# Token term of a graph layer: two small matmul groups on TensorE, or rows gathered from a table in DRAM

## The chip, the core and the metric

The kernel runs on one core of one Trainium2 chip. The metric is the device time of one execution in microseconds (us). TensorE is called PE in the profile, VectorE is DVE, ScalarE is ACT, GpSimd is POOL, and SyncE (SP) issues the kernel's transfers.

## The reference, cut to what matters

There are 64 sequences of 256 tokens, 768 wide. The adjacency is 0 or 1 with a mean of 1/64.

```
h    = relu(layernorm(x))
deg  = adj.sum(-1);  rdeg = adj.sum(1)            # both directions
ctx  = adj @ (h Wadj' + badj) / max(deg,1) + adj' @ (h Wrev' + brev) / max(rdeg,1) + h Wself' + bself
rel  = deg * (E[1] Wr' + br) + rdeg * (E[41] Wrr' + brr)      # for adjacencies of 0 and 1
out  = x + ctx + rel
```

For one token, everything that isn't a product with `h` is a sum of five rows of 768 elements: `badj` if deg > 0, `brev` if rdeg > 0, `bself`, deg times one vector, and rdeg times another. This is the token term. It depends on the two degrees alone.

## The kernel before

A sequence has two blocks of 128 tokens (c = 0, 1). The three weight products are computed in float32r words by a scheme of 15 products instead of 18 (`PRODUCTS`), in two sweeps over the sequences: sweep 1 runs 8 products for each of the 62 regular sequences and stores the partial blocks to DRAM (`kept`); sweep 2 loads them, runs the other 7 products and the aggregation with the adjacency, and stores the output. Sequences 0 and 63 are irregular: their products are taken whole, in full precision, at the start and at the junction of the sweeps. The junction also prepares the second set of weight words.

`record` writes every operation into a `Plan` with an engine, a planned duration and a rank; `Plan.schedule` is a list scheduler that runs at build time and fixes the order on each engine. The ranks are moved by a table of `OFFSETS`, one per kind of operation. Large tiles of 128x768 live in 18 rotating buffers (class B). All transfers go through SP's one queue. Engines work in order.

The parts around the change:

- `front1` (sweep 1): layernorm's statistics end in 4 columns of a tile `cols`: mean and variance of each block; GpSimd takes the power -1/2 (L721). TensorE turns the tile (L724), ScalarE copies 4 rows out of PSUM (L727), SP stores them to a DRAM tile `d` (L731) and loads them back broadcast as `row` (L734), with which GpSimd and VectorE normalise the transposed tokens (L743, L747).
- `rows_prepare` (at the junction): builds a tile `rows` of the five token-term rows, high and low parts, four times in groups of 32 partitions.
- `front2` (sweep 2): ScalarE converts the adjacency and sums the degrees (L896); VectorE writes indicator and degree columns into `cols` (L908, L909); TensorE turns them (L913); ScalarE copies them to `token` (L917).
- `add_rows` (L638): four matmuls with 32 rows each, on four row groups of TensorE, add the token term into the PSUM banks of products 7 and 15 (chains v and u), which are then read by VectorE into blocks (0, 1) and (1, 1). In the irregular sequences it has banks of its own, and VectorE adds them (L979).
- `product` reads a bank into the blocks it feeds (L685, L687); `high_low` splits finished blocks for the aggregation (ScalarE L926, GpSimd L930); `aggregate` multiplies (L942) and VectorE adds the result, divided by the degree, into blocks (c, 1) (L953).
- `split` makes the three words of a left operand (ScalarE L600, VectorE L613 and L617), from sums that GpSimd makes (L590).
- `flag`: a general path runs if any adjacency value is neither 0 nor 1.

## Time and profile before

| | |
|---|---|
| three timed runs | 2492.59, 2494.84, 2495.69 us (median 2494.84) |
| profiled execution, span | 2494.7 us |
| TensorE busy | 2467.6 us, 99% |
| VectorE, ScalarE, GpSimd busy | 84%, 72%, 52% |
| transfers | 590.67 MB, mean 237 GB/s, all on SP's queue |

The span reaches from the first to the last instruction of the profiled execution; its own device time isn't listed apart, and the span is within 0.1% of the runs. Busy time counts an engine's instructions, not its waits. Matmuls are pipelined, so a row's duration overlaps the next one; differences of start times tell what a group takes.

### The profile page before, as it was taken

Reading aid. Unit: us, or ns where it says so; the run is one execution under the profiler, and the core shown is the slowest. Engines: PE = TensorE matmul, PEld = TensorE weight load, DVE = VectorE, ACT = ScalarE, POOL = GpSimd, SP = SyncE. Lnnn points to the kernel's source line nnn. Section 1 sums busy time; section 2 is a strip of 40 time slices with the busy share of each in tenths; the row PEclk is TensorE's granted clock in tenths of the full one; section 3 lists DMA queues with packets and bytes.
Section 4 is the critical chain, followed back from the end, with each engine's and each line's share of the span. In section 5 each row is a group of like instructions: output and inputs, shape, how many; then the busy total and the mean of one; then the engine's idle time right before and its main releaser. Section 6 shows DMA issues by size and latency. Waiting matters only on the chain.

```text
span 2494.7 us, 43472 instructions
## 1 busy us (share of the span) xinstructions
PE 2467.6 (99%) x13922; PEld 2381.1 (95%) x13922; DVE 2091.7 (84%) x3939; ACT 1787.1 (72%) x3836; POOL 1285.3 (52%) x1138
## 2 busy tenths in 40 slices
PE   7999999999999999999999999999999999999998
PEld 4899999999999999996999999999999999999998
DVE  7887787777777777778988988888888888888887
ACT  3788888888888888886666666666666666666664
POOL 1555555555555555552555555555555555555554
PEclk9999999999999999999999999999999999999999
DMA  5677777777777677776666666666666666666663
GB/s 211 235 285 266 269 281 268 268 277 271 267 282 278 260 276 282 276 274 231 209 215 216 213 212 213 213 214 213 214 214 215 215 215 216 215 215 215 213 219 130
DMA packets 224009, 590.67 MB, mean 237 GB/s; under 512 B 24056, under 2 KB 24312, under 8 KB 223776
## 3 DMA queue, kind: packets, MB, share of 16 engines
q1 hardware_dynamic: 223776, 587.86, 67.3%
q8 instruction: 110, 1.80, 0.3%
q14 instruction: 123, 1.01, 0.1%
HBM read 364.28 MB, written 223.48 MB: 236 GB/s over the span
## 4 chain that ended last, share of the span: by engine, by line
PE 96%; DMA 1%; DVE 1%; ACT 1%; issue 0%; POOL 0%; SPq 0%; DVEq 0%; ACTq 0%; POOLq 0%
PE x L628 21%; PE y L628 20%; PE agg L942 14%; PE z L628 10%; PE w L628 10%; PE t L628 5%; PE v L628 5%; PE u L628 5%; PE whole L780 2%; PE v L638 1%; DMA raw<-in_Wadj_dram 0%; DMA raw<-in_Wself_dram 0%; PE right L502 0%; PE pt L724 0%; DVE right L555 0%
## 5 line engine op out<-in xcount | busy, mean ns | idle before, releaser
L930 POOL TENSOR_TENSOR hl<-c,hl 128x768 fp32r<-128x768 f32 x256 | 475.3, 1857 | 649.3 <-ACT hl L926 459.2
L628 PE MATMUL x<-word,left 128*128 128x384 f32 x2976 | 592.2, 340 | 0.2 <-DVE c L687 0.2
L628 PE MATMUL y<-word,left 128*128 128x384 f32 x2976 | 573.1, 337 | 0.0
L628 PEld LDWEIGHTS x<-word,left 128*128 128x128 f32 x2976 | 517.4, 188 | 14.2 <-issue 11.0
L628 PEld LDWEIGHTS y<-word,left 128*128 128x128 f32 x2976 | 521.4, 188 | 5.3 <-ACT y L666 0.6
L942 PE MATMUL agg<-hl,a 128*128 128x384 f32 x2048 | 395.4, 335 | 0.0
L743 POOL TENSOR_TENSOR h<-h,row 128x768 f32<-128x768 f32 x128 | 235.7, 1863 | 266.5 <-DMA row<-d 217.3
L942 PEld LDWEIGHTS agg<-hl,a 128*128 128x128 f32 x2048 | 358.5, 188 | 0.5 <-issue 0.2
L628 PE MATMUL w<-word,left 128*128 128x384 f32 x1488 | 304.2, 339 | 1.4 <-DVE x L791 1.3
L628 PE MATMUL z<-word,left 128*128 128x384 f32 x1488 | 301.3, 337 | 0.2
L666 ACT ACTIVATE x<-x 128x768 f32<-128x768 f32 x248 | 191.8, 794 | 140.1 <-PE x L628 139.9
L628 PEld LDWEIGHTS z<-word,left 128*128 128x128 f32 x1488 | 260.4, 188 | 3.4 <-ACT c L676 0.4
L628 PEld LDWEIGHTS w<-word,left 128*128 128x128 f32 x1488 | 258.3, 188 | 4.5 <-DVE x L791 1.6
L953 DVE SCALAR_TENSOR_TENSOR c<-agg,rd,c 128x768 f32<-128x768 f32 x252 | 255.0, 1012 | 7.3 <-PE agg L942 4.0
L926 ACT ACTIVATE hl<-c 128x768 fp32r<-128x768 f32 x256 | 215.1, 841 | 32.1 <-DVE c L685 24.3
L666 ACT ACTIVATE y<-y 128x768 f32<-128x768 f32 x248 | 197.3, 796 | 44.4 <-PE y L628 44.4
L617 DVE SCALAR_TENSOR_TENSOR left<-left,top 128x256 fp32r<-128x256 f32 x496 | 199.2, 412 | 6.3
L617 DVE SCALAR_TENSOR_TENSOR left<-left 128x256 fp32r<-128x256 f32 x434 | 203.0, 489 | 0.1
L685 DVE TENSOR_TENSOR c<-c,v 128x768 f32<-128x768 f32 x124 | 117.3, 946 | 101.5 <-PE v L628 100.5
L607 ACT ACTIVATE top<-left 128x256 f32<-128x256 f32 x496 | 181.2, 383 | 6.6 <-DVE left L617 2.6
L721 POOL TENSOR_TENSOR cols<-cols,half 128x2 f32<-128x2 f32 x64 | 83.9, 1311 | 152.9 <-DVE cols L720 152.9
L676 ACT ACTIVATE c<-y 128x768 f32<-128x768 f32 x124 | 100.9, 814 | 71.7 <-PE y L628 71.7
(138 smaller groups left out, 4343.8 us busy)
## 6 DMA issues: line engine op xcount, KB each, us to landing
c<-kept SPq DMA_DIRECT2D x316, 384.0 KB
kept<-c SPq DMA_DIRECT2D x252, 384.0 KB
x<-in_x_dram SPq DMA_DIRECT2D x128, 384.0 KB
h<-in_x_t_dram SPq DMA_DIRECT2D x128, 384.0 KB
out_dram<-c SPq DMA_DIRECT2D x126, 384.0 KB
kept_h<-h SPq DMA_DIRECT2D x124, 384.0 KB
h<-kept_h SPq DMA_DIRECT2D x124, 384.0 KB
adj<-in_adj_dram SPq DMA_DIRECT2D x64, 512.0 KB
```

Of the source, the lines that this page charges most:

```text
L607: lambda: nc.scalar.activation(view(top), t(w)[:, 0].bitcast(F32), AF.Copy),
L617: lambda: nc.vector.scalar_tensor_tensor(t(w)[:, 2], t(w)[:, 1].bitcast(F32), -STEP, first(), op0=ALU.mult, op1=ALU.add), s == 1,
L628: nc.tensor.matmul(t(q)[:, half, : H // 2], t(w)[:, lw, f, :], t(r[rw])[:, f, ts(half, H // 2)], start=start and i == 0 and f == 0, stop=s ...
L666: lambda: nc.scalar.activation(view(), view(), AF.Copy, scale=scale),
L676: lambda o=o, sign=sign: nc.scalar.activation(t(o).rearrange("p (k n) -> p k n", k=2), view(), AF.Copy, scale=sign * (1.0 if value_last el ...
L685: emit = lambda to=to, op=op: nc.vector.tensor_tensor(to(), to(), view(), op=op)
L721: pool(0.7, r - 21.5, f"pow {b}", [col], [col], lambda: nc.gpsimd.tensor_tensor(var(), var(), v["half"], op=ALU.pow))
L743: lambda h=h, one=one: nc.gpsimd.tensor_tensor(t(h), t(h), one(0), op=ALU.subtract),
L926: lambda: nc.scalar.activation(t(pair)[:, 0], t(o), AF.Copy, scale=LOWER),
L930: lambda: nc.gpsimd.tensor_tensor(t(pair)[:, 1], t(o), t(pair)[:, 0].bitcast(F32), op=ALU.subtract),
L942: nc.tensor.matmul(t(q)[:, half, : H // 2], t(s["a"])[:, c, k, ts(ic, P)], t(pairs[c])[:, part, ts(half, H // 2)], start=(c == 0 and part ...
L953: lambda q=q, to=to, ic=ic: nc.vector.scalar_tensor_tensor(to(), t(q)[:, :, : H // 2], t(rd)[:, ic, k : k + 1], to(), op0=ALU.mult, op1=AL ...
```

## The change

The token term comes from a table in DRAM of 1024 rows, one for each pair of degrees below 32. `table_prepare` builds it during sweep 1, from the fifth sequence on, one step for each of 12 sequences (`PACE_TABLE` is 17 us): the two weight vectors by matmuls, the bias rows loaded broadcast to 128 partitions, 14 VectorE operations on 128x768, and 8 stores of 128 rows. In `front2`, VectorE makes a row number 32 deg + rdeg for each token (place, index), and for each of the two blocks GpSimd issues an indirect transfer that adds the 128 rows numbered by the index to block (c, 1) in SBUF. The token columns, their turn, their copy, the token-row matmuls and `rows_prepare` go. The reads of the banks of products 7 and 15 no longer wait for the rows.

The statistics are turned by VectorE, which transposes 32x32 squares: the four columns stand 8 apart in a tile of 128x32, and the store to `d` picks every eighth partition. The general path also runs if a degree is 32 or more. The planner gets the gather's planned times (1.2 us on GpSimd and on the queue, 3.5 us to land), and the `OFFSETS` are replaced as a whole (not shown).

```diff
+SPAN = 32
...
+PACE_TABLE = 17.0
+GATHER = 3.5
...
+                elif o.name.startswith("gather"):
+                    idle[e] = o.end
+                    queue = max(queue, now) + 1.2
+                    o.end += GATHER
...
-    def add_rows(b, rank, token, qs, start):
...
-        pe(0.55, rank, f"token rows {b}", [token, v["rows"], *qs], [*qs], run)
...
-        if s == 0 or n not in (7, 15):
-            for i in range(len(reads)):
-                read(i)
-            return
-        read(0)
-        return q, lambda: read(1)
+        for i in range(len(reads)):
+            read(i)
...
+        four = lambda: t(col).rearrange("p (c k e) -> p c k e", c=C, k=2)[:, :, :, 0]
...
-        pt = plan.buf("U", None, None, f"pt_{b}", inside=hold)
-        line = plan.buf("S", [P, P], F32, f"line_{b}")
-        pe(0.3, r - 20.0, f"turn {b}", [col], [pt], lambda: nc.tensor.transpose(t(pt)[:, :P], t(col), v["ident"]))
-        act(
-            0.27, r - 19.5, f"line {b}", [pt], [line],
-            lambda: nc.scalar.activation(t(line)[:4], t(pt)[:4, :P], AF.Copy),
-        )
+        line = plan.buf("S", [P, 32], F32, f"line_{b}")
+        dve(0.17, r - 19.5, f"line {b}", [col], [line], lambda: nc.vector.transpose(t(line), t(col)))
         d = plan.buf(None, None, None, "d", v["dram"].tile([4, P], F32, tag="d", name=f"d_{b}"))
         row = plan.buf("A", [P, 4, P], F32, f"row_{b}")
-        dma(2, r - 19.0, f"d {b}", [line], [d], lambda: nc.sync.dma_start(t(d), t(line)[:4]))
+
+        def spread():
+            nc.sync.dma_start(
+                t(d).rearrange("k (q j) -> q k j", q=4), t(line).rearrange("(m e) j -> m e j", e=8)[:, 0]
+            )
+
+        dma(2, r - 19.0, f"d {b}", [line], [d], spread)
...
+    def table_prepare(rank):
+        table = v["table"]
+        pick = plan.buf("B", [P, H], F32, "pick")
         wr = [plan.buf("B", [P, H], F32, f"wr{k}") for k in range(2)]
+        vec = [plan.buf("B", [P, H], F32, f"vec{k}") for k in range(2)]
+        base = plan.buf("B", [P, H], F32, "base")
+        rev = plan.buf("B", [P, H], F32, "rev")
+        fwd = plan.buf("B", [P, H], F32, "fwd")
+        cols = plan.buf("S", [P, 16], F32, "table_cols")
+        for q in range(P // SPAN):
+            at = slice(SPAN * q, SPAN * (q + 1))
+
...
+            pool(0.6, rank - 9.0, "count", [], [(cols, q)], count)
...
         dma(40, rank - 8.0, "eT", [], [(pick, 9)], lambda: nc.sync.dma_start(t(pick)[:, 2 * P : 2 * P + NREL], v["e_t"]))
+        step = PACE_TABLE
         for k in range(2):
+            dma(384, rank - 8.0 + step * k, "wr", [], [wr[k]], lambda k=k: nc.sync.dma_start(t(wr[k]), v["wr"][k]))
+        for i, (r, to) in enumerate(((3, vec[0]), (4, vec[1]), (2, base), (1, rev), (0, fwd))):
+            dma(
+                384, rank - 7.0 + step * i, "bias", [], [to],
+                lambda r=r, to=to: nc.sync.dma_start(t(to), v["bias"][r].partition_broadcast(P)),
+            )
...
+        for k in range(2):
+            pr = plan.buf("Q", [P, 2, 512], F32, f"pr{k}")
+
+            def picks(k=k, pr=pr):
+                for n in range(2):
                     nc.tensor.matmul(
+                        t(pr)[:, n, : H // 2], t(pick)[:, k * P : (k + 1) * P], t(wr[k])[:, ts(n, H // 2)], start=True, stop=True
                     )
 
+            pe(1.45, rank - 4.0 + step * k, "pick", [(pick, k), wr[k]], [pr], picks)
+            dve(
+                on_dve(H), rank - 3.0 + step * k, "vec", [pr, vec[k]], [vec[k]],
+                lambda k=k, pr=pr: nc.vector.tensor_tensor(
+                    t(vec[k]).rearrange("p (k n) -> p k n", k=2), t(vec[k]).rearrange("p (k n) -> p k n", k=2),
+                    t(pr)[:, :, : H // 2], op=ALU.add,
+                ),
+            )
+
+        def add(name, at, one, col, to, out=None):
+            out = out or to
+            dve(
+                on_dve(H), at, name, [one, cols, to], [out],
+                lambda: nc.vector.scalar_tensor_tensor(
+                    t(out), t(one), t(cols)[:, col : col + 1], t(to), op0=ALU.mult, op1=ALU.add
+                ), True,
+            )
+
+        add("base", rank + 2.0 * step, vec[1], 8, base)
+        add("base", rank + 3.0 * step, rev, 9, base)
+        for i in range(SPAN * SPAN // P):
+            tile_ = plan.buf("B", [P, H], F32, f"table{i}")
+            at = rank + (4.0 + i) * step
+            if i == 0:
+                add(f"table {i}", at, fwd, 10, base, tile_)
+                add(f"table {i}", at, vec[0], i, tile_)
+                dve(
+                    on_dve(H), at + 1.0, "base", [base, fwd], [base],
+                    lambda: nc.vector.tensor_tensor(t(base), t(base), t(fwd), op=ALU.add), True,
+                )
+            else:
+                add(f"table {i}", at, vec[0], i, base, tile_)
+            dma(
+                384, at + 2.0, "table", [tile_], [(table, i)],
+                lambda tile_=tile_, i=i: nc.sync.dma_start(t(table)[ts(i, P), :], t(tile_)),
+            )
...
-        col, rd = v["cols"][b % 2], v["rd"][b % 2]
+        rd = v["rd"][b % 2]
         degs = [(deg, (b, c, k)) for c in range(C) for k in range(2)]
...
-        dve(0.2, r - 2.0, f"tok {b}", degs, [(col, 0)], lambda: nc.vector.tensor_scalar(to(0), of(), 0.0, None, op0=ALU.is_gt))
-        dve(0.2, r - 2.0, f"tok {b}", degs, [(col, 1)], lambda: nc.vector.tensor_copy(to(3), of()))
+        place = plan.buf("S", [P, 2 * C], F32, f"place_{b}")
+        index = plan.buf("S", [P, C], I32, f"index_{b}")
+        dve(
+            0.2, r - 2.0, f"place {b}", degs, [place],
+            lambda: nc.vector.tensor_scalar(
+                t(place), t(deg)[:, b].rearrange("p c k -> p (c k)"), 0.0, float(SPAN - 1), op0=ALU.max, op1=ALU.min
+            ),
+        )
+
+        def index_of():
+            one = lambda k: t(place).rearrange("p (c k) -> p c k", k=2)[:, :, k]
+            nc.vector.scalar_tensor_tensor(t(index), one(0), float(SPAN), one(1), op0=ALU.mult, op1=ALU.add)
+
+        dve(0.2, r - 1.5, f"index {b}", [place], [index], index_of)
         dve(0.2, r - 2.0, f"rd {b}", degs, [rd], lambda: nc.vector.tensor_scalar(t(rd), t(deg)[:, b], 1.0, None, op0=ALU.max))
         dve(0.2, r - 2.0, f"rd {b}", [rd], [rd], lambda: nc.vector.reciprocal(t(rd), t(rd)))
-        pt = plan.buf("Q", [P, 2, 512], F32, f"pt2_{b}")
-        pe(0.3, r - 1.0, f"turn2 {b}", [col], [pt], lambda: nc.tensor.transpose(t(pt)[:, 0, :P], t(col), v["ident"]))
-        s["token"] = v["tokens"][b % 2]
...
+        for c in range(C):
+            o = blocks[b, c, 1]
+            plan.op(
+                "POOL", 1.2, r + 1.0 + 2.0 * c, f"gather{c} {b}", [index, o, v["table"]], [o],
+                lambda o=o, c=c: nc.gpsimd.indirect_dma_start(
+                    t(o), None, t(v["table"]), IndirectOffsetOnAxis(ap=t(index)[:, c : c + 1], axis=0), compute_op=ALU.add
+                ),
+            )
         return s
...
-        held = []
         for i, spec in enumerate(SWEEPS[1] if b in regular else ()):
-            more = product(b, 1, spec, r + 2.1 * i, banks)
-            if more:
...
-        if b not in regular:
...
+            product(b, 1, spec, r + 2.1 * i, banks)
...
+        table_prepare(start1[4])
         front1(B - 1)
         whole(B - 1, 1, last)
-        rows_prepare(last + 20.0)
...
+        dve(
+            0.5, start2[B - 2] + 1.0, "rest", [deg, rest], [deg],
+            lambda: nc.vector.tensor_scalar(t(deg), t(deg), float(SPAN), None, op0=ALU.is_ge),
+        )
+        most = plan.buf("S", [P, 1], F32, "most")
         dve(0.4, start2[B - 2] + 1.0, "total", [rest], [total], lambda: nc.vector.tensor_reduce(t(total), t(rest), AX.XY, ALU.add))
+        dve(
+            0.5, start2[B - 2] + 1.0, "total", [deg], [most],
+            lambda: nc.vector.tensor_reduce(t(most), t(deg).rearrange("p b c k -> p b (c k)"), AX.XY, ALU.add),
+        )
+        dve(
+            0.2, start2[B - 2] + 1.0, "total", [total, most], [total],
+            lambda: nc.vector.tensor_tensor(t(total), t(total), t(most), op=ALU.add),
+        )
...
-            "cols": [own(f"cols{i}", [P, P], F32) for i in range(2)],
-            "tokens": [own(f"token{i}", [P, P], F32R) for i in range(2)],
+            "cols": [own(f"cols{i}", [P, 32], F32) for i in range(2)],
+            "table": plan.buf(None, None, None, "table", keep.tile([SPAN * SPAN, H], F32, name="table")),
```

## Rows read from the trace of the kernel before

**Rows 1.** The page's part 1, busy us (share of the span) xinstructions.

```profile
PE 2467.6 (99%) x13922; PEld 2381.1 (95%) x13922; DVE 2091.7 (84%) x3939; ACT 1787.1 (72%) x3836; POOL 1285.3 (52%) x1138
```

**Rows 2.** The page's part 4, the chain that ended last, by engine.

```profile
PE 96%; DMA 1%; DVE 1%; ACT 1%; issue 0%; POOL 0%; SPq 0%; DVEq 0%; ACTq 0%; POOLq 0%
```

**Rows 3.** Windows of one sequence: PE, PEld, DVE, ACT, POOL busy, clock, DMA share, GB/s.

```profile
130.00:146.90 16.90, 16.90 (x99) 16.82 (x98) 13.42 (x30) 14.17 (x29) 8.87 (x9) 1.00 0.74 277
...
1556.00:1576.90 20.90, 20.90 (x123) 20.43 (x122) 18.48 (x33) 13.48 (x33) 10.95 (x9) 1.00 0.65 214
```

**Rows 4.** TensorE in order of time, sweep 2: start us, us, engine, line.

```profile
1555.06 1.55 PE L942 MATMUL agg<-hl,a 128*128 128x384 f32 x8
...
1570.36 0.27 PE L913 MATMUL pt<-ident,cols 128*128 128x128 f32 x1
...
1571.89 0.85 PE L628 MATMUL u<-word,left 128*128 128x384 f32 x4
1572.58 1.55 PE L942 MATMUL agg<-hl,a 128*128 128x384 f32 x8
1574.06 0.44 PE L638 MATMUL v<-rows,token 32*128 32x384 f32 x2
...
1575.95 1.55 PE L942 MATMUL agg<-hl,a 128*128 128x384 f32 x8
```

**Rows 5.** Line 638: duration ns min/median/max, first and last start us.

```profile
L638 PE MATMUL v<-rows,token x124: 434/436/439, 1201.3 to 2473.2; 32*128 32x384 f32 x124
```

**Rows 6.** TensorE in order of time, sweep 1.

```profile
1085.07 0.87 PE L628 MATMUL z<-word,left 128*128 128x384 f32 x4
1085.78 0.27 PE L724 MATMUL pt<-ident,cols 128*128 128x128 f32 x1
...
1086.59 1.58 PE L628 MATMUL y<-word,left 128*128 128x384 f32 x8
```

**Rows 7.** TensorE in order of time, the junction.

```profile
1159.75 0.96 PE L638 MATMUL rows<-rows,token 32*128 32x384 f32 x4
1160.64 5.43 PE L780 MATMUL whole<-raw,h 128*128 128x384 f32 x16
```

**Rows 8.** All engines in order of time, the start.

```profile
6.74 0.71 POOL L721 TENSOR_TENSOR cols<-cols,half 128x2 f32<-128x2 f32 x1 [5.42 <-DVE cols L720]
...
8.30 0.34 SPq L731 DMA_DIRECT2D d<-line  x1
...
11.41 0.36 SPq L734 DMA_DIRECT2D row<-d  x1
```

**Rows 9.** Groups by line: busy us, mean ns of one, idle before.

```profile
L930 POOL TENSOR_TENSOR hl<-c,hl 128x768 fp32r<-128x768 f32 x256 | 475.3, 1857 | 649.3 <-ACT hl L926 459.2 <-DMA c<-in_x_dram 176.9 <-issue 13.2
...
L617 DVE SCALAR_TENSOR_TENSOR left<-left 128x256 fp32r<-128x256 f32 x434 | 203.0, 489 | 0.1
...
L720 DVE TENSOR_SCALAR cols<-cols 128x2 f32<-128x2 f32 x64 | 10.6, 165 | 1.0
```

**Rows 10.** Lines 617 and 721: duration ns min/median/max, first and last start.

```profile
L617 DVE SCALAR_TENSOR_TENSOR left<-left x434: 396/414/787, 1175.9 to 2472.3; 128x256 fp32r<-128x256 f32 x145
...
L721 POOL TENSOR_TENSOR cols<-cols,half x64: 699/1340/1383, 6.7 to 1103.3; 128x2 f32<-128x2 f32 x64
```

**Rows 11.** All engines in order of time, sweep 2, around the degrees.

```profile
1564.41 0.19 ACT L896 ACTIVATION_READ_ACCUMULATOR a<-adj 128x1 f32 x1
...
1568.36 0.17 DVE L908 TENSOR_SCALAR cols<-deg 128x16 f32<-128x16 f32 x1
...
1570.62 0.95 DVE L685 TENSOR_TENSOR c<-c,v 128x768 f32<-128x768 f32 x1 [1.73 <-PE v L628]
...
1572.09 0.96 DVE L687 SCALAR_TENSOR_TENSOR c<-x,c 128x768 f32<-128x768 f32 x1 [0.52 <-PE x L628]
```

**Rows 12.** All engines in order of time, sweep 1, around one broadcast.

```profile
124.34 0.38 SPq L734 DMA_DIRECT2D row<-d  x1
...
129.60 3.65 POOL L743 TENSOR_TENSOR h<-h,row 128x768 f32<-128x768 f32 x2 [3.55 <-DMA row<-d]
```

More of the change, by code (lines that the diff above doesn't have):

```diff
@@ L6 @@
 from concourse import mybir
-from concourse.bass import ts
+from concourse.bass import IndirectOffsetOnAxis, ts
 from concourse.masks import make_identity
@@ L632, in passes @@
                     )
-    def add_rows(b, rank, token, qs, start):
-        def run():
-            for g in range(4):
-                at = slice(32 * g, 32 * (g + 1))
-                nc.tensor.matmul(
-                    t(qs[g // 2])[:, g % 2, : H // 2], t(token)[at], t(v["rows"])[at, ts(g % 2, H // 2)],
-                    start=start, stop=True, skip_group_check=not start, tile_position=(32 * g, 0),
-                )
-        pe(0.55, rank, f"token rows {b}", [token, v["rows"], *qs], [*qs], run)
     def product(b, s, spec, rank, banks):
@@ L858, in rows_prepare @@
-        dve(
-            on_dve(H), rank - 1.0, "rows", [rest, hi, upper], [rows],
-            lambda: nc.vector.scalar_tensor_tensor(
-                t(rows), t(hi).bitcast(F32), t(upper)[:, 1:], t(rest), op0=ALU.mult, op1=ALU.add
-            ), True,
-        )
+            pe(1.45, rank - 4.0 + step * k, "pick", [(pick, k), wr[k]], [pr], picks)
[6 more added lines that the diff above has]
+            )
@@ L960, in step2 @@
         r = start2[b]
-        held = []
         for i, spec in enumerate(SWEEPS[1] if b in regular else ()):
-            more = product(b, 1, spec, r + 2.1 * i, banks)
-            if more:
-                held.append(more)
-            if len(held) == 2:
-                add_rows(b, r + 2.1 * i + 3.0, s["token"], [q for q, _ in held], False)
-                for _, read in held:
-                    read()
-                held = []
-        if b not in regular:
-            qs = [plan.buf("Q", [P, 2, 512], F32, f"rows{c}_{b}") for c in range(C)]
-            add_rows(b, r, s["token"], qs, True)
-            for c in range(C):
-                o = blocks[b, c, 1]
-                to = lambda o=o: t(o).rearrange("p (k n) -> p k n", k=2)
-                dve(
-                    on_dve(H), r + c + 1.0, f"rows{c} {b}", [qs[c], o], [o],
-                    lambda q=qs[c], to=to: nc.vector.tensor_tensor(to(), to(), t(q)[:, :, : H // 2], op=ALU.add),
-                )
+            product(b, 1, spec, r + 2.1 * i, banks)
         at = lambda x: r + (x if b in regular else 0.5 * x - 2.0)
```

81 lines of the change are left out of this document (20 added, 61 removed), and 273 rows, old and new, of the table OFFSETS.

## The prediction

> **What bounds the kernel now.** I read the page first: TensorE is busy for 99% of the span [rows 1], and the chain of waits that ended last runs through it for 96% [rows 2]. Then the table of windows, one window as long as one sequence from each sweep [rows 3]: TensorE fills its 16.9 us of sweep 1 and its 20.9 us of sweep 2 without a gap, at the full granted clock (its level of 2.4 GHz), while VectorE has 13.4 of 16.9 and 18.5 of 20.9, GpSimd about 9 and 11, and the DMA engines are busy for 0.74 and 0.65 of the time. So in both sweeps a microsecond counts only if it comes off TensorE's queue, or if another engine becomes so late that TensorE waits. The third view, TensorE's order of time, says what a sequence of sweep 2 is made of [rows 4]: from 1555.06 to 1570.36 it starts 88 product and aggregate matmuls, 15.30 us, 0.1739 us each. A sequence has 84 + 32 = 116 of these, 20.17 us. The token-row matmuls occur 124 times a bank, two for each of 62 sequences, from 1201.3 to 2473.2 [rows 5]: 61 steps of 20.85 us. The 0.68 us between 20.85 and 20.17 are the token term.
>
> **What comes off TensorE.** The same rows show it by pieces. The turn and the 8 matmuls behind it take 1571.89 - 1570.36 = 1.53 us, 8 x 0.1739 = 1.39 of them matmuls: the turn costs 0.14. Between the aggregate's start at 1572.58 and the token rows at 1574.06 lie 1.48 us for 8 matmuls, a wait of 0.09. From the token rows to the next aggregate at 1575.95 lie 1.89 us with 8 matmuls between, so the four row matmuls cost 0.50 [rows 4]. Sum 0.73, against 0.68 by the pace; I take 0.70, times 62 = 43 us. In sweep 1 the statistics' turn and 4 matmuls take 0.81 us where 4 alone take 0.71 [rows 6]: 0.10, times 62 = 6 us. At the junction the four token-row matmuls of one irregular sequence hold 0.89 us [rows 7], some of it a wait; with the other sequence and two turns I count 1.5 us. The small matmuls that make the bias vectors stay eight in number and only move into sweep 1, so they cost nothing more.
>
> At the start the statistics lie on the path: GpSimd's power ends at 6.74 + 0.71 = 7.45 and the row store is issued at 8.30 [rows 8]. A VectorE transpose of 128x32 is not in the trace; the bounds are 0.17 us, the small VectorE op of the same tile, and 0.41, an op on 256 columns [rows 9, 10]. I take 0.25, near the small one, and gain 0.4 us. Together 43 + 6 + 1.5 + 0.4 = 51 us.
>
> **What is added, and what hides it.** *Sweep 1:* 63 transposes x 0.17 to 0.41 are 11 to 26 us on VectorE, 0.25 us a sequence of the 3.5 that it has free [rows 3]. They also wait for GpSimd's power, 1.34 us [rows 10], with the splits and bank reads of the running sequence queued behind them; 1.34 + 0.25 fits into 3.5, so nothing is charged. Without that room it would be 1.6 x 62 = 99 us. ScalarE only loses work. The store of the turned rows has 16 short pieces instead of 4 rows; it stays one issue on SP's queue, and I leave its landing as it is.
>
> *The table:* 14 VectorE ops on 128x768, each about the 0.96 us of such an op [rows 11], 14 us over 12 sequences, again inside the free 3.5 us. Eight small counting ops on GpSimd, at most 8 x 1.34 = 11 us, before any of it is needed. SP issues 15 more transfers of 384 KB, two of which (the weights) come from the junction; at one or two a sequence they add 0.4 to 0.8 MB to the 4.6 that the window moves at 0.74 busy. The dear resource is room: vectors and table pieces hold four to eight of the 18 large buffers. Bounds: nothing, or one 0.96 us op's length for each of 12 steps, 12 us; I take 2. The three more VectorE ops for the flag are behind the last degrees: nothing to 3 x 0.41, I take 0.5.
>
> *Sweep 2:* VectorE gives up two small ops and gets two (place, index) of the same 0.17 us [rows 11]: nothing. It is then busy 18.5 of 20.2 us. ScalarE loses a copy. GpSimd gets two gathers. No GpSimd DMA is in the trace. Its time on the engine is bounded by the 1.34 us of a tiny GpSimd op and the 1.86 us of one on 128x768 [rows 9, 10]; I take 1.34, since it handles 128 indices. That is 2.7 us a sequence, 13.7 of 20.2 with the low halves queued behind, which have the rest as room. Its landing is bounded by the smallest transfer, 11.41 - 8.30 = 3.11 us with little else in flight [rows 8], and by the broadcast of 256 KB in sweep 1, issued at 124.34 and consumed at 129.60, 5.26 us [rows 12], times 1.5 for 384 KB, 7.9. I take 5.3, the loaded case. A gather then takes 1.3 + 5.3 = 6.6 us, 4.5 to 9.8 at the ends.
>
> Is that in time? The degrees are complete at 1564.60; the first add into a gathered block is at 1572.09 [rows 11]. With 0.33 us for place and index, 7.15 us remain if VectorE takes the two up at once: 6.6 fits, with half a microsecond over. If it takes them up where the token columns stand now, at 1568.36, only 3.4 us remain. But VectorE idles 1.73 and 0.52 us in just this stretch, waiting for TensorE [rows 11], so up to 2.2 us of lateness fall into holes. I take the hidden case and charge 1 us in all for odd late ones.
>
> The Trainium skill (DMA: Bandwidth & Descriptors, section "Anatomy of one DMA — SWDGE (gpsimd) path") fits such a transfer with 2.0 us plus its bytes at 436 GB/s, 2.9 us for 384 KB as an estimate. With that in place of 5.3 the gather takes 4.2 us and the sum does not change. No run here shows it, and the loaded row stands above it.
>
> **Sum.** The profiled span is 2494.7 us, 0.1 under the median of the runs (2494.84, 2492.59 to 2495.69). 2494.7 - 51 + 2 + 0.5 + 1 = 2447, which I round to 2446 since the pieces gave 0.73 and the pace 0.68. The likeliest case's own range is 2438 (0.73 a sequence, no charge) to 2456 (table at 12 us).
>
> **Rivals.** *Late gathers (slower).* Place: VectorE's first add into the gathered block, with the bank reads behind it, for which the next products on TensorE wait. With place and index at 1568.36 and 6.6 us, the block is 6.6 - 3.4 = 3.2 us late, 1.0 beyond the holes: 62 us on 2446 is 2508. At 9.8 us it would be 4 us, far worse; at 4.5 nothing. It decides from 49 / 62 = 0.8 us beyond the holes. For it: the lookup starts only after the degrees, whereas the token rows needed no transfer. Against it: 7.15 us are there for the taking.
>
> *VectorE becomes the bound (a part of the gain).* It has 18.5 us of work, and waits of 2.2 us for single products [rows 11]. If these don't shrink, the pace is 20.7 instead of 20.85: 9 us there, 6 in sweep 1 and 2 elsewhere, 2478.
>
> *The DMA engines hold the old pace.* 214 GB/s x 20.9 us are 4.5 MB; the gathers add 0.8, or 1.6 if the read of the destination counts. 5.3 to 6.1 MB in 20.2 us are 260 to 300 GB/s, against 277 in sweep 1 at 0.74 [rows 3], so I hold it unlikely. Then only sweep 1 and the junction gain: 2487.
>
> *GpSimd and VectorE shut each other out.* The two-input op on 128x256 takes 0.489 in the mean and 0.414 in the median, 0.787 at most [rows 9, 10]: some wait on something, 0.5 us a sequence for 10.9 us of GpSimd work, so two gathers would add a tenth. But if a gather held VectorE for 1.86 us, twice a sequence, VectorE would need 18.5 + 3.7 = 22.2: 62 x 1.35 = 84 us over the old pace, 2571. The Trainium skill (SBUF — State Buffer, section "SBUF: two separate sides") has the rule: the two engines share a port pair by an exclusive lock, and a GpSimd DMA's descriptors can't be written while VectorE holds it in a two-port mode. In sweep 2 the trace has no large VectorE copy of that kind, and GpSimd at half load delays VectorE little, so the rows bear the rule out only weakly.
>
> *It doesn't do what it says:* a degree of 32 or more would send everything through the general path. The mean degree is 256/64 = 4; I give that nothing.
>
> **Chances.** Likeliest 0.45; VectorE 0.15; DMA 0.05; late gathers 0.29, of which 0.03 are small enough to stay faster, 0.06 end within 0.2%, 0.20 slower; shutting out 0.06. Faster by over 0.2% (about 5 us, what a measurement here can tell): 0.68, within: 0.06, slower: 0.26. The range reaches from 2437 to 2520: that leaves out 0.03 below and 0.16 above, the worse half of the late gathers and the shutting out.
>
> **What would show it.** Right: steps of 20.1 to 20.3 us in sweep 2 and 16.8 in sweep 1, no wait of TensorE, VectorE's waits for single products shorter, no wait of VectorE for a GpSimd transfer. Wrong: VectorE's adds into the c tiles waiting for a transfer from the table, with gaps on TensorE behind them; low halves waiting on GpSimd; GpSimd idle before gathers because block loads are late; sweep 1 losing time between the fifth and the sixteenth sequence; a DMA share near 1 in sweep 2.

## The result, and the profile after

The changed kernel takes 3003.68 us (2997.72 to 3006.89), the kernel before 2494.53 in the same runs: a ratio of 1.2035, 95% interval 1.2021 to 1.2049. The forecast was 2446, range 2437 to 2520. The profiled span is 3004.2 us.

The page of the changed kernel, its parts 1, 3 and 4: busy time, GpSimd's own DMA queue, and the chain that ended last.

```profile
PE 2599.1 (87%) x13538; PEld 2497.4 (83%) x13538; DVE 2137.9 (71%) x3996; ACT 1784.9 (59%) x3706; POOL 1450.3 (48%) x1272
...
q0 software_dynamic: 18432, 50.34, 10.6%
...
PE 62%; issue 14%; POOL 10%; DVE 5%; DMA 5%; ACT 3%; POOLq 0%; ACTq 0%; DVEq 0%; SPq 0%
```

TensorE fell from 99% to 87% [rows 1], and the chain is no longer its own: "issue", time in which an engine waits for nothing that the profile names, has 14%, where before TensorE had 96% [rows 2]. No engine is full, so nothing has become the bound by its work; something waits. The table of windows, a stretch of each sweep:

```profile
520.00:820.00 300.00, 299.63 (x1692) 293.28 (x1692) 245.76 (x531) 248.32 (x493) 152.57 (x158) 1.00 0.76 274
1460.00:1860.00 400.00, 321.68 (x1644) 316.74 (x1643) 260.43 (x452) 192.45 (x431) 198.52 (x156) 0.89 0.67 186
```

Sweep 1 keeps its pace nearly (against [rows 3]). Sweep 2 has TensorE idle a fifth of the time and a mean granted clock of 0.89, between its two levels; the DMA share is 0.67, so the transfers are not short of engines. Product u's matmuls, which occur in sweep 2 alone, run from 1236.8 to 2974.7: 28.5 us for each of 61 steps, where [rows 5] had 20.85. One sequence in order of time, all engines, shows the mechanism (start, duration, engine, instruction; in brackets the idle time before and what ended it):

```profile
2004.12 1.58 POOL L939 DMA_INDIRECT c<-table,index  x1 [0.53 <-DVE index L930]
...
2011.54 0.96 DVE L672 SCALAR_TENSOR_TENSOR c<-x,c 128x768 f32<-128x768 f32 x1 [2.76 <-DMA c<-table,index]
2011.95 1.56 POOL L939 DMA_INDIRECT c<-table,index  x1 [6.26 <-issue]
...
2012.93 1.33 POOL L586 TENSOR_TENSOR a0+a<-h 128x256 f32<-128x256 f32 x1
2013.62 2.40 POOL L954 TENSOR_TENSOR hl<-c,hl 128x768 fp32r<-128x768 f32 x1
2014.30 0.42 ACT L596 ACTIVATE left<-a0+a 128x256 fp32r<-128x256 f32 x1 [6.82 <-POOL a0+a L586]
...
2016.08 1.01 PE L966 MATMUL agg<-hl,a 128*128 128x384 f32 x2 [5.65 <-POOL hl L954]
...
2016.88 2.76 PE L624 MATMUL x<-word,left 128*128 128x384 f32 x8
2017.72 0.95 DVE L670 TENSOR_TENSOR c<-c,u 128x768 f32<-128x768 f32 x1 [4.36 <-DMA c<-table,index]
```

The first gather is issued at 2004.12. The second one, next on GpSimd, starts 6.26 us after the first has left the engine, just behind the first one's landing (VectorE's add into its block starts at 2011.54). GpSimd works in order, so the sum a0+a and the low half stand behind it; ScalarE waits 6.82 us for the sum and TensorE 5.65 us for the low half. Then 8 matmuls take 2.76 us instead of 1.55: from 2014.9 to 2021.6 the granted clock is 0.50, the lower level of 1.2 GHz; it fell within the gap of 5.65 us. The gather's line by itself: its idle time by what ended it, who waited for it, and its landing, counted from the end of its time on GpSimd.

```profile
L939 POOL DMA_INDIRECT c<-table,index x126: 1552/1568/2530, 1191.0 to 2979.0; - x126
...
  issue: 225.9, 42
...
  DVE c L670: 140.1, 33
  DVE c L672: 107.8, 55
...
DMA to landing us min/median/max: 5.3/5.7/8.6
```

TensorE's two largest waits of sweep 2 (1237 to 2975 us: us in all, times, longest):

```profile
PE agg L966 <- POOL hl L954: 181.3, 32, 7.0
PE v L624 <- ACT v L651: 154.6, 30, 6.3
```

The first is the low half; for the second, ScalarE scales product v, and ScalarE itself waits 386 us in all for the sum a0+a. Besides, the granted clock is 0.50 for 394 us of sweep 2, and for 4 us where the gathers are left out (e2 below).

### The profile page after: what moved, and what is told of

It reads as the page before. It is cut to its first block, busy times and chain, and to the rows that moved or that the text cites. A ratio compares the mean times of both kernels' runs of the same rounds, so it can differ in the third digit from the quotient of the medians.

```text
span 3004.2 us, 43259 instructions
## 1 busy us (share of the span) xinstructions
PE 2599.1 (87%) x13538; PEld 2497.4 (83%) x13538; DVE 2137.9 (71%) x3996; ACT 1784.9 (59%) x3706; POOL 1450.3 (48%) x1272
## 4 chain that ended last, share of the span: by engine, by line
PE 62%; issue 14%; POOL 10%; DVE 5%; DMA 5%; ACT 3%; POOLq 0%; ACTq 0%; DVEq 0%; SPq 0%
PE y L624 15%; PE x L624 12%; PE agg L966 11%; PE z L624 8%; PE w L624 7%; POOL c L939 5%; PE t L624 4%; PE whole L763 3%; POOL hl L954 2%; POOL a0+a L586 2%; PE v L624 2%; DMA h<-kept_h 1%; DMA adj<-in_adj_dram 1%; DVE left L613 1%; DVE left L609 1%
## 5 line engine op out<-in xcount | busy, mean ns | idle before, releaser
L954 POOL TENSOR_TENSOR hl<-c,hl 128x768 fp32r<-128x768 f32 x256 | 525.3, 2052 | 383.3 <-ACT hl L950 363.4
L966 PE MATMUL agg<-hl,a 128*128 128x384 f32 x2048 | 477.3, 379 | 192.9 <-POOL hl L954 182.8
L624 PE MATMUL x<-word,left 128*128 128x384 f32 x2976 | 631.1, 359 | 3.9 <-DVE c L672 1.9
L966 PEld LDWEIGHTS agg<-hl,a 128*128 128x128 f32 x2048 | 424.4, 221 | 206.2 <-POOL hl L954 194.2
L624 PEld LDWEIGHTS x<-word,left 128*128 128x128 f32 x2976 | 581.7, 207 | 6.7 <-ACT x L651 2.6
L939 POOL DMA_INDIRECT c<-table,index x126 | 199.4, 1583 | 410.9 <-issue 221.4
L624 PE MATMUL v<-word,left 128*128 128x384 f32 x744 | 172.4, 371 | 155.9 <-ACT v L651 154.6
L670 DVE TENSOR_TENSOR c<-c,u 128x768 f32<-128x768 f32 x124 | 118.1, 953 | 248.9 <-DMA c<-table,index 140.1
L624 PEld LDWEIGHTS v<-word,left 128*128 128x128 f32 x744 | 143.2, 208 | 165.9 <-ACT v L651 164.2
L596 ACT ACTIVATE left<-a0+a 128x256 fp32r<-128x256 f32 x62 | 25.8, 416 | 386.1 <-POOL a0+a L586 386.1
```

The costliest lines, as they stand in the source:

```text
L624: nc.tensor.matmul(t(q)[:, half, : H // 2], t(w)[:, lw, f, :], t(r[rw])[:, f, ts(half, H // 2)], start=start and i == 0 and f == 0, stop=s ...
L670: emit = lambda to=to, op=op: nc.vector.tensor_tensor(to(), to(), view(), op=op)
L939: lambda o=o, c=c: nc.gpsimd.indirect_dma_start(t(o), None, t(v["table"]), IndirectOffsetOnAxis(ap=t(index)[:, c : c + 1], axis=0), comput ...
L954: lambda: nc.gpsimd.tensor_tensor(t(pair)[:, 1], t(o), t(pair)[:, 0].bitcast(F32), op=ALU.subtract),
L966: nc.tensor.matmul(t(q)[:, half, : H // 2], t(s["a"])[:, c, k, ts(ic, P)], t(pairs[c])[:, part, ts(half, H // 2)], start=(c == 0 and part ...
```

## The experiments

Medians in us, and where the profiled execution ends sweep 1 (last start of product z's matmuls) and runs sweep 2 (first and last of product u's):

| run | time | z to | u from, to | u's length |
|---|---|---|---|---|
| before | 2495 | 1121.2 | 1194.3, 2470.9 | 1276.6 |
| after | 3004 | 1151.1 | 1236.8, 2974.7 | 1737.9 |
| e1 room 2048 | 2789 | 1151.2 | 1232.3, 2762.8 | 1530.5 |
| e2 no gathers | 2522 | 1152.4 | 1224.1, 2495.5 | 1271.4 |
| e3 written, not added | 2613 | 1153.4 | 1231.4, 2579.4 | 1348.0 |
| e4 one gather | 2670 | 1150.9 | 1231.9, 2634.0 | 1402.1 |
| e5 before, no token rows | 2472 | 1120.7 | 1193.5, 2447.1 | 1253.6 |
| e6 before, VectorE's turn | 2498 | 1117.5 | 1191.6, 2474.3 | 1282.7 |
| e7 room, bound on ScalarE | 2755 | 1151.4 | 1233.8, 2729.0 | 1495.2 |
| e8 gathers late | 2761 | 1154.1 | 1224.5, 2728.9 | 1504.4 |
| e9 GpSimd busy, no transfer | 2596 | 1152.1 | 1225.7, 2572.1 | 1346.4 |
| e11 no gathers, no table | 2514 | 1140.2 | 1213.6, 2484.5 | 1270.9 |
| e12 room 576 | 2798 | 1150.6 | 1233.2, 2765.4 | 1532.2 |
| e13 planner told, TensorE's turn | 2987 | 1152.2 | 1234.8, 2965.2 | 1730.4 |
| e14 e8 without gathers | 2577 | 1148.8 | 1219.2, 2545.8 | 1326.6 |
| e15 e13 without gathers | 2716 | 1149.8 | 1223.4, 2683.0 | 1459.6 |
| e16 e8, low halves written | 2535 | 1152.8 | 1223.9, 2499.2 | 1275.3 |
| e17 e7, low halves written | 2819 | 1150.8 | 1228.9, 2793.5 | 1564.6 |

### Room for two gathers, no gathers, other gathers

**e1: more room.**

```diff
-dynamic_dma_scratch_size=512
+dynamic_dma_scratch_size=2048
```

> Only the room reserved for GpSimd's transfers grows, from 512 to 2048 bytes of each SBUF partition; the order of every engine stays. Theory A (room): in the changed kernel the second gather of a sequence finds no room while the first is in flight, so GpSimd stands for some 6 us with its sums and low halves queued behind it. Then the idle time ahead of gathers that waits for nothing the profile shows falls from 226 us to under 20, the second gather starts right after the first, and the time falls by 400 to 550 us, to 2450 to 2600. Rival B (one at a time): GpSimd puts down an indirect transfer only after the one before has landed, whatever the room: time stays at 3000, the idle time at 226. Rival C (late landing): GpSimd's idle time goes, but the time falls by no more than about half, to 2700 to 2800, because VectorE's adds go on waiting for the 5.7 us landings.

2788.59 us, ratio to before 1.1172 (1.1153 to 1.119): 215 us less. GpSimd's "issue" idle time ahead of gathers fell from 225.9 to 8.1 us. So A's standing GpSimd is confirmed and B falls; but the time is above A's range and near C's, so something else stays. In order of time:

```profile
2014.82 1.58 POOL L939 DMA_INDIRECT c<-table,index  x1 [0.31 <-issue]
...
2015.82 1.36 POOL L586 TENSOR_TENSOR a0+a<-h 128x256 f32<-128x256 f32 x1
...
2016.52 2.46 POOL L954 TENSOR_TENSOR hl<-c,hl 128x768 fp32r<-128x768 f32 x1
2017.13 4.39 DVE L933 TENSOR_SCALAR rd<-deg 128x4 f32<-128x4 f32 x1
...
2018.33 1.33 POOL L586 TENSOR_TENSOR a0+a2+b<-a0+a,h 128x256 f32<-128x256 f32 x1
2019.02 2.40 POOL L954 TENSOR_TENSOR hl<-c,hl 128x768 fp32r<-128x768 f32 x1
...
2021.44 0.94 DVE L672 SCALAR_TENSOR_TENSOR c<-x,c 128x768 f32<-128x768 f32 x1
...
2022.44 1.68 PE L624 MATMUL x<-word,left 128*128 128x384 f32 x8 [2.77 <-DVE c L672]
```

The second gather now follows the first. But a VectorE op on 128x4, 0.16 us in the changed kernel, takes 4.39: it ends 0.1 us behind the second low half, and an add, and TensorE behind it, waits for VectorE. That is GpSimd shutting VectorE out. The Trainium skill (SBUF — State Buffer, section "SBUF: two separate sides") has it as an exclusive lock on a shared port pair, against VectorE ops in a two-port mode or with two SBUF inputs; this row agrees in that a tensor_scalar is held; in which mode it ran, the profile doesn't say. The splits, which have two SBUF inputs, are hardly held here: 0.44 and 0.43 us in the mean in their two largest groups.

**e12: just enough room.** The same edit with 576.

> The changed kernel with 576 instead of 512 bytes of room. 128 adding gathers left 18432 packets, 9 on each of 16 DMA engines for one gather; if a gather takes two places of 16 bytes for each of them, two need 36 places, and 512 bytes have 32. By that count of theory A 576 are enough: within 15 us of the run with 2048 bytes (2789). If a gather needs more, the second one still waits: 2950 to 3005.

2797.59 (2796.09 to 2799.09), near e1; idle "issue" 6.0 us. The limit lies between 512 and 576 bytes, where the count in the expectation puts it; the number and the size of its places are shown by nothing else.

**e2: no gathers.**

```diff
-lambda o=o, c=c: nc.gpsimd.indirect_dma_start(...),
+lambda: None,
```

> Both gathers are left out and nothing else, so the output lacks the token term; table, row numbers, VectorE's turn and the order on each engine stay. If the gathers alone carry the loss (A, B and C alike): TensorE's steps of 20.1 to 20.3 us in sweep 2 and a time of 2440 to 2452, the sum of the prediction without its charge for late gathers. If the table or VectorE's turn of the statistics costs something in sweep 1 or at the junction (rival D): 2455 to 2480, with TensorE's gaps before the gathers begin.

2521.91, ratio 1.0104 (1.0087 to 1.012): slower than before without a single gather, and above D's range too. Sweep 1 ends 31 us later than before, and sweep 2 takes 1271.4 instead of 1276.6: 5 us gained where 43 were forecast. Ahead of GpSimd's power in sweep 1 stands the op that adds epsilon:

```profile
L702 DVE TENSOR_SCALAR cols<-cols x64: 155/678/978, 6.2 to 1116.7; 128x2 f32<-128x2 f32 x64
```

Its median is 0.68 us, where it needs 0.16.

**e3 and e4: no adding, and one gather.**

```diff
-IndirectOffsetOnAxis(...), compute_op=ALU.add
+IndirectOffsetOnAxis(...)
```

> The gathers write their rows over the block instead of adding them, so that products in the block are lost; room 512 as in the changed kernel. If adding takes twice the places of a plain gather (a branch of A: 32 places of 16 bytes a partition in 512), both plain gathers fit, GpSimd no longer stands and the time is within 50 us of the run with more room. If the second gather waits for the first to land in any case (B), or a plain gather needs the same room, the time stays within 100 us of 3000.

2612.96: no standing GpSimd (10.4 us of "issue"), and better than e1 by 176, outside of what either reading expected. A plain gather is cheaper in each respect: 0.96 us on GpSimd instead of 1.57, 80 packets for 144, a landing of 5.2 us in the median for e1's 7.6, and the sums behind it keep their length (0.75 in the mean).

```diff
-lambda o=o, c=c: nc.gpsimd.indirect_dma_start(...),
+lambda o=o, c=c: None if c else nc.gpsimd.indirect_dma_start(...),
```

> Only the gather into block 0 is left; block 1 gets no token term. A and B alike: the transfer of the sequence before has long landed when the next is issued (20 us apart), GpSimd never stands, and the time is 2445 to 2520. Rival E (each gather by itself holds up GpSimd and VectorE while it is in flight): half of the loss stays, some 2720.

2670.27: 148 over e2, more than half of e1's 267 over it. GpSimd doesn't stand; VectorE waits 78.2 us for this one landing, and the largest group of its two-input splits takes 0.70 us in the mean. A single gather in this place is too dear already.

### The parts alone

**e5: before without the token rows.**

```diff
-pe(0.55, rank, f"token rows {b}", ..., run)
+pe(0.55, rank, f"token rows {b}", ..., run if start else lambda: None)
```

(and the turn and its copy likewise)

> The kernel before without its token term in the 62 regular sequences: their turn of the token columns, its copy and the token-row matmuls are left out, nothing else, the order stays. The prediction's first term stands alone here: 0.70 us a sequence off TensorE is 43 us, so 2450 to 2456. Rival (VectorE holds the pace once TensorE is lighter): 2475 to 2485. If the time lies there, the changed kernel's 20.7 us steps without any gather have the same cause.

2472.08, ratio 0.9905 (0.9888 to 0.9921): 24 us, a little over half of the 43. A step is 20.55 us, not 20.17. What came off TensorE comes back partly around one aggregate, 0.32 us a step by start times, most of it ahead of the aggregate, as in this wait of its weight load:

```profile
1609.09 1.36 PEld L943 LDWEIGHTS agg<-hl,a 128*128 128x128 f32 x8 [0.36 <-PE x L628]
```

**e6: before with VectorE's turn.**

```diff
-pe(0.3, ..., f"turn {b}", ...); act(0.27, ..., f"line {b}", ...)
+dve(0.17, r - 19.5, f"line {b}", [col], [line], lambda: nc.vector.transpose(t(line), t(col)))
```

> The kernel before with the statistics turned by VectorE, and nothing else of the change; the planner orders anew with the old offsets. The prediction counted a gain of 6 us and no charge: 2487 to 2490. Rival (F): in the changed kernel the op that adds epsilon takes 0.68 us in the median instead of 0.16, behind a GpSimd op, and TensorE loses 0.3 to 0.4 us a sequence behind a late bank read. If VectorE's turn as such brings this, the time is 2500 to 2520.

2498.22, ratio 1.0008 (0.9999 to 1.0018), between both. Sweep 1 ends 3.7 us earlier, against 6 forecast, and the op that adds epsilon takes 0.161 in the median, so F falls: in the old order VectorE's turn costs nothing. Sweep 2, which it doesn't touch but which was ordered anew, takes 6 us more.

**e11: no gathers, no table.** As e2, with the steps of the table recorded and not emitted.

> The run without gathers (2522), and besides, nothing of the table is built: its small matmuls, the 14 VectorE ops, its loads and stores are left out; the order stays. The prediction charged 2 us for the table (0 to 12). In the traces TensorE starts its matmuls between 120 and 330 us some 19 us late in all against the kernel before. If that is the table (rival D): 2500 to 2508. If it is the tightened order around it: 2515 to 2522.

2513.72: the table is worth 8 us of the time; sweep 1 ends 12.2 us earlier. Neither reading as put: 19 of the 31 us of sweep 1 are left. They look like VectorE's turn, with its late epsilon op, but e13 and e15 below speak against it. They turn the statistics on TensorE again and keep the table; the epsilon op is back near its own length (here e15), and sweep 1 still ends at 1152.2 and 1149.8:

```profile
L1330 DVE TENSOR_SCALAR cols<-cols x64: 155/170/1780, 6.2 to 1125.7; 128x2 f32<-128x2 f32 x64
```

So the 19 us go with the changed order, whose `OFFSETS` were replaced as a whole, on whichever engine the turn is; what in the order makes them wasn't taken apart.

### What holds the gathers' run at 2789

**e7: the lower bound on ScalarE.** With e1's room:

```diff
-dve(..., nc.vector.tensor_scalar(t(rd), t(deg)[:, b], 1.0, None, op0=ALU.max))
+act(..., nc.scalar.activation(t(rd), t(deg)[:, b], AF.Copy, bias=1e-30))
```

> The run with more room (2789), and one op moved besides: the degrees' lower bound, a VectorE tensor_scalar of 128x4 that took 159 us in 64 instances there, 5.4 us at most, becomes a ScalarE op that adds 1e-30. Theory G (GpSimd shuts VectorE out while it works off sums and low halves behind the gathers): the time falls by 80 to 150 us to 2640 to 2710, and no VectorE op waits on its own for more than 1.5 us. Rival C (late landing): the wait only moves to the adds into the gathered blocks, and the time falls by less than 40 us.

2755.12: 33 less, C's side. The op's 159 us of VectorE are gone, and the adds wait for the table's transfer instead, 194 us in all against 82 in e1. The hold had lain in front of the landing. Who waits for the gathers, their landing, and TensorE's two largest waits of sweep 2:

```profile
  DVE c L672: 109.5, 36
  DVE c L670: 84.1, 40
DMA to landing us min/median/max: 5.4/7.6/9.5
...
PE agg L966 <- DVE c L670: 68.5, 48, 3.0
PE x L624 <- DVE c L672: 57.1, 29, 3.3
```

So in this order most of what is left over e2 runs through the landing: TensorE's two largest waits stand behind just these adds.

**e8: the gathers late.** e7, and:

```diff
 # step2, behind aggregate(b, s, 0, ...)
+for c in range(C):
+    plan.op("POOL", 1.6, at(23.0 + 1.4 * c), f"gather{c} {b}", ..., indirect_dma_start(..., compute_op=ALU.add))
 for c in range(C): dma(384, at(24.0), f"out{c} {b}", ...)
```

> As the run before it, with the gathers moved behind the last VectorE op on their block, just ahead of the store of the output (the sum is the same in another order), so that no engine waits for a landing; the planner counts 1.6 us for the issue and 5.5 for the landing. If landing and the shutting out carry what is left over the run without gathers (2522): 2505 to 2550. If GpSimd's own load, 1.6 us a gather and the slower sums beside a transfer in flight, is dear by itself (rival E): 2580 to 2650, with TensorE waiting for sums and low halves.

2761.42: no gain, far above both ranges, though nothing but the store of the output waits for a landing. In order of time, VectorE and GpSimd:

```profile
2017.30 1.64 POOL L991 DMA_INDIRECT c<-table,index  x1 [0.88 <-DVE left L613]
2017.42 0.42 DVE L609 TENSOR_TENSOR left<-a0+a2+b,left 128x256 fp32r<-128x256 f32 x1
2017.76 3.68 DVE L613 SCALAR_TENSOR_TENSOR left<-left 128x256 fp32r<-128x256 f32 x2
2018.38 2.43 POOL L947 TENSOR_TENSOR hl<-c,hl 128x768 fp32r<-128x768 f32 x1
...
2023.84 2.46 POOL L947 TENSOR_TENSOR hl<-c,hl 128x768 fp32r<-128x768 f32 x1
...
2024.30 2.35 DVE L609 TENSOR_TENSOR left<-h,left 128x256 fp32r<-128x256 f32 x1
```

A split with two SBUF inputs, 0.42 us, runs beside a gather, but one that meets a low half is held until that ends, and then runs: 2.35 us, and 3.68 for two that need 0.75. In this order the splits come when the low halves do.

**e9: GpSimd busy without a transfer.**

```diff
-lambda o=o, c=c: nc.gpsimd.indirect_dma_start(...),
+lambda: nc.gpsimd.tensor_tensor(busy, busy, busy, op=ALU.subtract),   # 128x636
```

> Each gather of the changed kernel is replaced by a GpSimd op without any transfer, a subtract on 128x636 elements of a tile of its own, some 1.57 us by the rows of 256 and 768 elements (0.74 and 1.86 us); so the token term is left out. Beside the run without gathers (2522) it shows what GpSimd's time and its hold on VectorE cost, without room and landing. Theory G (GpSimd's longer runs of work shut VectorE's two-input ops out, and its sums and low halves come later): 2570 to 2700. Rival C (landing and room are all): 2520 to 2545.

2595.52, ratio 1.0398 (1.038 to 1.0415): 74 us over e2, G's side: a GpSimd op in this place costs more than a microsecond a sequence with no transfer at all. As a likeness of a gather it is off in two ways. It takes 1.33 us in the mean and not 1.57; and it reads SBUF and holds the splits, which a gather doesn't: in e1 the 205 splits that overlap a gather and nothing else of GpSimd's take 0.42 us in the mean, 0.48 at most.

**e13: the planner told.** Room 1024, TensorE's turn, and in the scheduler:

```diff
-GATHER = 3.5
+GATHER = 5.7
+SLOWED = 0.59
...
-    o.end += GATHER
+    o.end += GATHER + (1.9 if now < flight else 0.0)
+    flight = max(flight, o.end)
+elif e == "POOL" and now < flight:
+    o.end += SLOWED
...
```

(the gather is locked against VectorE's two-input ops; offsets of sweep 2 searched anew; the gather's planned time on GpSimd stays at 1.2 us, not the 1.58 that the expectation names)

> The changed kernel with 1024 bytes of room, the statistics turned by TensorE as before, and a planner that is told what the runs showed: a gather takes 1.58 us of GpSimd and shuts VectorE's two-input ops out like any GpSimd op, lands 5.7 us later (7.6 with another one in flight), and GpSimd's ops beside it take 0.59 us more. The offsets of sweep 2 are searched anew against that plan. Theory H (room apart, the loss is a plan made with 1.2 and 3.5 us, whose order drifts into VectorE's and GpSimd's shutting each other out): 2510 to 2580, most of the 290 us over the kernel before gone, though not below it, since a gather's 1.58 us and its slower neighbours stay. If no order helps against landing and shutting out (C, G): above 2680.

2987.33 (2956.35 to 2999.2): this plan doesn't help, and H's forecast fails. It isn't a full test of H, since the plan still counts 1.2 us for a gather, takes GpSimd as slower beside one, which it isn't (last section), and has gathers hold splits. VectorE is busy longer than in the changed kernel, 2484.4 us against 2137.9, and one of its splits of 0.42 us takes 2.01 at 2012.57, 18 us after the last gather left GpSimd.

**e14 to e17: the order or the gathers, the hold or the landing.** e14 and e15 are e8 and e13 with the gathers' edit of e2; e16 and e17 are e8 and e7 with

```diff
-lambda: nc.gpsimd.tensor_tensor(t(pair)[:, 1], t(o), t(pair)[:, 0].bitcast(F32), op=ALU.subtract),
+lambda: nc.gpsimd.memset(t(pair)[:, 1].bitcast(F32), 0.0),
```

> The run with late gathers (2761), in its own order, with both gathers left out (no token term). Nothing lands there that an engine waits for, so it shows what of its 240 us over the run without gathers (2522) is the transfer and what the order. If the gathers' time on GpSimd and the slower ops beside them push VectorE's splits into GpSimd's low halves (G by the gathers): 2505 to 2545. If the new order meets in that way by itself (I): above 2650.

2576.76: between both readings. The late order alone costs 55 us over e2; the gathers in it the other 185.

> The run whose planner was told the measured times (2987), in its own order, with both gathers left out (no token term). G by the gathers: 2510 to 2570. The order by itself (I): above 2850, with VectorE's two-input splits held for 2 us and more though nothing is in flight.

2715.55: again between, 194 us over e2 by order alone (with TensorE's turn), and the gathers 272 more. One group of splits takes 1.14 us in the mean where 0.42 is its length, with nothing in flight.

> The run with late gathers (2761), with GpSimd's low halves replaced by writing zeros into the same 128x768 places, which reads nothing of SBUF and shuts no two-input op out as far as theory G goes; so the low halves' part of the aggregation is left out. G: VectorE's splits of 128x256 are back at 0.42 us in the mean (0.85 and 1.3 in two groups there), and the time falls to 2510 to 2600. If the splits are held by the gathers or their transfers (E): they stay above 0.7, and the time above 2680.

2535.01, ratio 1.0155 (1.0138 to 1.0172): 226 us less than e8, G. The same groups in e8 (first fence) and e16 (second):

```profile
L613 DVE SCALAR_TENSOR_TENSOR left<-left 128x256 fp32r<-128x256 f32 x434 | 357.7, 847 | 2.1
...
L609 DVE TENSOR_TENSOR left<-h,left 128x256 fp32r<-128x256 f32 x124 | 164.6, 1327 | 0.0
```

```profile
L613 DVE SCALAR_TENSOR_TENSOR left<-left 128x256 fp32r<-128x256 f32 x434 | 179.6, 437 | 2.1
...
L609 DVE TENSOR_TENSOR left<-h,left 128x256 fp32r<-128x256 f32 x124 | 52.5, 423 | 0.3 <-ACT left L596 0.3
```

These splits are near their own length, with both transfers still there. Added up over sweep 2, the splits that write to `left` take 328 us over their 0.42 us each in e8, and 32 in e16. The time is even 42 us under e14, which has no gathers. A GpSimd op that only writes doesn't hold a split: 114 that overlap such writes alone take 0.42 us in the mean, and those still held overlap a sum, which reads (the same section of the Trainium skill limits the lock against two-input ops to a GpSimd op that reads SBUF; the runs agree). The write is also shorter than the low half, 1.05 us in the mean for 2.13 in e8, so some of the 226 us may be GpSimd's time.

> The run with more room and the lower bound on ScalarE (2755), with the same replacement of the low halves by zeros. What is left is the landing of 5.7 to 7.6 us behind 1.6 us of GpSimd, with VectorE's adds waiting. C (landing is the larger part of what is left): 2640 to 2730. G (GpSimd's hold was the larger part): 2530 to 2600.

2818.69, above both ranges and 64 over e7: in this order the hold is not what limits. There was little of it to take: 18 us over all splits in e7, 13 here. The add waits by itself:

```profile
2006.49 0.95 DVE L670 TENSOR_TENSOR c<-c,u 128x768 f32<-128x768 f32 x1 [4.22 <-DMA c<-table,index]
2007.36 1.01 DVE L977 SCALAR_TENSOR_TENSOR c<-agg,rd,c 128x768 f32<-128x768 f32 x1
2007.60 2.90 PE L966 MATMUL agg<-hl,a 128*128 128x384 f32 x8 [3.54 <-DVE c L670]
```

The two groups of adds wait 137.2 and 112.3 us for the landing (median 8.1), 56 us more than in e7, nearly the 64 by which the time rose. Why the landing is later wasn't settled.

## Why the prediction was wrong

**The step that failed** is "That is 2.7 us a sequence, 13.7 of 20.2 with the low halves queued behind, which have the rest as room". It counted the gathers' own time on GpSimd, and that was nearly right (1.57 for 1.34, and the next op starts 0.99 us behind a gather's start). What it left out is that the second gather can't be put down while the first has the room, so that GpSimd stands for a landing with the sums and low halves behind it. e1 and e12 show it: 215 and 206 us. The prediction named no rival in which GpSimd itself waits for a transfer, though two gathers in a row on an engine that works in order, and the 512 bytes of room that the kernel reserves for them, were there to be asked about.

A second step failed with it: "I take the hidden case and charge 1 us in all for odd late ones". With room for both gathers the time is still 267 us over the run without them, and in e7 VectorE's adds wait 194 us in all for the landing.

**From 2446 to 3004**, step by step, as differences of runs: the saving alone ends at 2472, 26 over the forecast, of which 19 are the first term (24 us measured for 43). The changed order with VectorE's turn makes 42 (2514 - 2472). The table is 8 (2522 - 2514). The gathers with room for both are 267 (2789 - 2522), and the missing room 215. The sum is 558. Each is the price in that place and order; the runs show that a part's price changes with them.

**What comes off TensorE** was mis-sized: 0.70 us a sequence measured 0.38 (e5, u's length 23.0 us shorter over 61 steps). The pieces read from [rows 4] were right as time on TensorE, and 0.32 us a step comes back around an aggregate. The rival of a pace of 20.7 foresaw this size, with VectorE as its cause; the row in e5 shows a late aggregate, and which engine is behind it the profile doesn't say.

**Sweep 1.** The gain by VectorE's turn was right in sign (3.7 us for 6, e6). That nothing was charged for its place held in the old order. What the sum lacked is a term for the new order itself: 19 us in sweep 1, which stay when the turn goes back to TensorE (e13, e15). The table's 2 us were 8, inside the bounds of 0 to 12.

**The landing** was taken at 5.3 within 3.1 to 7.9; one measures 5.7, two in flight 7.6. A gather takes 7.3 us instead of 6.6, where 7.15 were available. No gather was in the trace when the term was made. The estimate of 2.9 us from the Trainium skill (DMA: Bandwidth & Descriptors, section "Anatomy of one DMA — SWDGE (gpsimd) path") is half of what the adding gather measures. The rival of late gathers is thereby true as well. Its condition (0.8 us beyond the holes) was met, its price of 62 us too low: in e7 the waits for the table alone are 194 us, with a landing of 7.6 in the median, and the granted clock is 0.50 in 30 stretches of sweep 2, 107 us together.

**GpSimd and VectorE shutting each other out** had 0.06, with the gather as the one who holds. The holder is another: the sums and low halves, which read SBUF. It isn't what the changed kernel pays. There, while GpSimd stands, the lower bound takes 0.16 us (4.39 in e1), and the splits of sweep 2 are 17 us in all over their 0.42 each, less than the 38 before. It shows where the order is another: 84, 154 and 188 us in e2, e14 and e15, which have no gather at all, and 328 in e8. The small delays in [rows 9, 10], 0.489 in the mean for 0.414, were its sign: before, 127 of 853 splits took over 0.6 us, each beside a reading GpSimd op. The rule of the Trainium skill (SBUF — State Buffer, section "SBUF: two separate sides") that VectorE can keep descriptors from being written shows in no row: an adding gather's time on GpSimd stays between 1.56 and 1.58 in the median throughout, and 4 of 128 in the changed kernel took over 1.7.

**No version found is faster than before.** The best run with both gathers and the whole computation is e7 with 2755; with the token term left out and nothing put in its place, e5 has 2472, 1% under before.

What stays open: how the 267 us divide between landing and hold, since each hides the other (e7 takes the hold off one op and brings up the landing; e8 takes the landing away and brings up the hold), though e7's rows speak for the landing; what in the new order costs the 19 us of sweep 1; and why the landing is later in e17.

## What to carry to other kernels

Before moving work to transfers that an engine puts down itself, ask how many fit in flight at once, and what stands behind the next one on that engine. In a kernel whose order is fixed in advance, a part's price is not its own duration alone: test the order with the part emitted as nothing, as e2, e14 and e15 do, before blaming the part. A new order needs a term of its own in the sum: here orders without a single gather cost between 27 and 220 us over the kernel before (e2, e14, e15).

## What the runs showed of the hardware

An adding gather of 128 rows of 3 KB takes GpSimd 1.57 us, with the next op starting 0.99 us behind its start, and leaves 144 packets; one that writes takes 0.96 and leaves 80. GpSimd ops that follow an adding gather without a gap end about 0.6 us later, whatever their size: 1.33 us for 0.74 on 128x256, 2.40 for 1.85 on 128x768, and 1.34 for 0.74 for writing zeros. The next op starts as early as ever, 0.69 us behind a sum and 1.77 behind a low half, so GpSimd's pace doesn't fall; what comes late is an op's end. The first gap undoes it, also with the transfer still in flight, in e1:

```profile
2038.98 1.55 POOL L939 DMA_INDIRECT c<-table,index  x1 [0.30 <-DVE left L613]
2039.97 1.33 POOL L586 TENSOR_TENSOR a0+a<-h 128x256 f32<-128x256 f32 x1
...
2042.44 1.34 POOL L586 TENSOR_TENSOR a0+a2+b<-a0+a,h 128x256 f32<-128x256 f32 x1
2043.86 0.74 POOL L586 TENSOR_TENSOR a0+a2+b0+b<-h,a0+a2+b 128x256 f32<-128x256 f32 x1
```

The last one stands 0.08 us behind the one before it and 3.3 behind the gather's end, where no gather of the run lands in less than 5.4. Of e1's ops of sweep 2 within 5.3 us of a gather's end, 244 of 246 without a gap since the gather are longer, and none of the 69 behind a gap. Behind plain gathers (e3) no op is longer: a0+a stays at 0.75.

Two adding gathers fit into 576 bytes of room, and not into 512. A VectorE tensor_scalar of 128x4 was held for up to 5.4 us by a row of GpSimd ops, with no gap for it between them.
